# An adaptive-norm block on one core: the opening of the first batch in a written-out issue order

## The chip, the core and the metric

The kernel runs on one core of one Trainium2 chip. The metric is the device time of one execution in microseconds (us), from the first to the last instruction with what lies around them; lower is better. All data are 32-bit floats. The engines are called TensorE (PE in the profile, its weight loads PEld), VectorE (DVE), ScalarE (ACT), GpSimd (POOL) and SyncE (SP). SyncE only issues transfers here; ScalarE and GpSimd issue some too.

## The reference

There are four batches of 512 tokens with 512 channels. In short:

```python
mod = (silu(c) @ wmod).reshape(4, 6, 1, 512)          # sa, ca, ga, sb, cb, gb
h = layernorm(x) * (1 + ca) + sa
q = silu(conv4(h @ Wq)); k = silu(conv4(h @ Wk)); v = silu(conv4(h @ Wv))   # 6 heads, 64/64/128
beta = sigmoid(h @ Wb); g = -exp(A_log) * softplus(h @ Wa + dt_bias)
o = gated_delta_rule(l2norm(q) * 64**-0.5, l2norm(k), v, g, beta)           # a scan over tokens
x = x + ga * ((rmsnorm(o) * norm_weight * silu(h @ Wg)) @ Wo)
h = layernorm(x) * (1 + cb) + sb
x = x + gb * ((silu(h @ w_gate.T) * (h @ w_up.T)) @ w_down.T)
```

## The kernel before

**Tiling.** A matrix of tokens and channels is held channels first, 128 channels by 512 tokens, so that one projection to 128 output channels is four accumulating matrix products with 512 columns (`projected`, L424). The profile counts each of them twice, so a whole projection shows as x8.

**Who sets the order.** The program is written against a framework with a scheduler: it knows the data dependencies, gives every instruction a priority from the place in the program, and writes one fixed order for each engine. On the chip each engine takes its instructions strictly in that order and waits where an operand isn't there. Tiles come from pools with a few buffers for each tag; a new tile waits until the oldest of its tag is done with. The tags that matter: `fill` and `seq` (three PSUM banks each), `w` (four projection weights), `acc` (four 128x512 results), `wm` (one buffer, for the later modulation weights and then for the weight sums), `sq` (one buffer).

**The opening of batch 0**, as the program has it:

- `modulation(*modulation_load(j))` for j = 1 and 0 (L227): the 1 MB weight is loaded on ScalarE's queue, multiplied (L188), copied from PSUM by VectorE (L190), reduced and turned over the channels by small products (L194), and added into `mod_t` (L195).
- `load_x(0)` on SyncE's queue; the sentinel writes of `far` into `gd` (L248, eight small transfers) also on SyncE's.
- `normed_t(0)`: statistics (L276, L277), the root on ScalarE (L286), normalising (L289, VectorE), 16 transposes (L295), and four scaled copies to `ht` on ScalarE (L296).
- `keys`, `queries`, `values` of batch 0: for each of 3 + 3 + 6 projections `conv_silu` does the product (L424), a scaled copy on ScalarE (L432), three tap additions on VectorE (L434) and the activation on ScalarE (L438). For keys and queries, `squares` follows (L444 on ScalarE, L450 on TensorE, L451).
- `decays` and `stored`: the decay gates of the delta rule, some thirty tiny VectorE operations, ending in a store to `gd`.
- `load_x(1)` and `load_x(2)` on ScalarE's queue; `normed_t` of both comes after `triangles(0)` in the program.

**What follows.** `triangles(0)` reads `gd` back (`ec`, L532), scans and exponentiates it, multiplies it onto products of the keys (L574, L578), stores the result (`ad`, L581), loads it in another layout (`pm`, L588) and inverts 96 small triangles in thirty dependent VectorE steps (L598, L602). The inverse is stored (`td`, L606) and read back as `t` (L651), and the first product of `delta_rule(0)` needs it (L659). The matrix products that fill TensorE during `delta_rule(0)` are `keys` and `queries` of batches 1 to 3 (`rest`). Later modulations run one at a time in `step`, between values: a 1x1 copy by GpSimd (`after`, L171) holds the load back, and L188, L190, then L194 or L198 follow.

**Weight sums.** `weight_sums` makes combinations of the feed-forward weights, sixteen times in sequence through the single `wm` buffer: load (L803, SyncE's queue), four sums on GpSimd (L808 to L811), store (L812). The weights of the projections of batches 1 to 3 are loaded on the same SyncE queue (L210), in between.

The line that puts the inversion ahead of everything for batch 0:

```python
with tc.high_priority(-LATER if b else 0):
```

Of the kernel before, what the change touches and what calls it, by code (L numbers as in the profile page):

```python
# [7 lines left out]

F32 = mybir.dt.float32
# [6 lines left out]
P = 128  # L16
# [21 lines left out]
def adaln_block(  # L38
# [40 lines left out]
    def fill(name):  # L79
        return bank("fill", 3, name)  # L80
# [76 lines left out]
    warm = const.tile([P, 1], F32, name="warm")  # L157
    act.activation(warm, eps, AF.Silu)
    act.activation(sc_t[:, :, :B], c_in, AF.Silu)

# [23 lines left out]
    def modulation(j, wm):  # L184

        pm = fill(f"pm{j}")
        for k in range(KD):
            pe.matmul(pm[k * S : (k + 1) * S, :], sc_t[:, k, :], wm[:, k, :], start=True, stop=True)  # L188
        part = pa_.tile([P, D], F32, tag="acc", bufs=4, name=f"part{j}")
        vec.tensor_copy(part, pm)  # L190
        if j in MOD:
            pt = fill(f"pmt{j}")[:, : KD * B].rearrange("p (t b) -> p t b", b=B)
            for t in range(KD):
                pe.matmul(pt[:, t, :], part[:, t * P : (t + 1) * P], fold[:, :B], start=True, stop=True)  # L194
            vec.tensor_scalar_add(mod_t[:, MOD[j]], pt, 1.0 if j in (1, 4) else 0.0)  # L195
            return
        pg = fill(f"pmg{j}")[:B, :]
        pe.matmul(pg, fold[:, :B], part, start=True, stop=True)  # L198
        val = pa_.tile([P, D], F32, tag="acc", bufs=4, name=f"val{j}")[:B]
        vec.tensor_copy(val, pg)  # L200
        mag = pa_.tile([P, D], F32, tag="acc", bufs=4, name=f"mag{j}")[:B]
        vec.scalar_tensor_tensor(mag, val, -1.0, val, ALU.mult, ALU.max)
        vec.tensor_scalar(val, val, 0.0, 2.0, ALU.is_ge, ALU.mult)
        vec.tensor_scalar_add(val, val, -1.0)
        vec.scalar_tensor_tensor(mag, mag, 0.25, val, ALU.max, ALU.mult)
        pool.dma_start(gate_d[j // 3], mag)

    def weight(src, col, nm):
# [4 lines left out]
    def load_x(b):  # L213
        ts = []
        if b == 2:

            room = w1.tile([P, NT, D], F32, tag="hf", bufs=2, name=f"xt{b}")
        for c in range(NT):
            if b == 2:
                t = room[:, c, :]  # L220
            else:
                t = pa_.tile([P, D], F32, tag="xt", bufs=4, name=f"xt{b}_{c}")
            (act if b else sp).dma_start(t, x[b, c * P : (c + 1) * P, :])
            ts.append(t)
        return ts

    for j in (1, 0):  # L227
        modulation(*modulation_load(j))
    first_w = weight(w_k, 0, "k0_0")
    xts = load_x(0)  # L230
    wab = const.tile([P, KD, S], F32, name="wab")
# [3 lines left out]
    for nm, src, n in (("k", conv_k, NP), ("q", conv_q, NP), ("v", conv_v, H)):  # L235
        cw[nm] = const.tile([P, n, TAPS], F32, name=f"conv_{nm}")
        sp.dma_start(cw[nm], src.rearrange("(n p) i -> p n i", p=P))
    neg_a = const.tile([P, H], F32, name="neg_a")
    sp.dma_start(neg_a, a_log.partition_broadcast(P))
    act.activation(neg_a, neg_a, AF.Exp)  # L240
    pool.tensor_scalar(neg_a, neg_a, -1.0, None, ALU.mult)
    dtb = const.tile([P, H], F32, name="dtb")
    sp.dma_start(dtb, dt_bias.partition_broadcast(P))
    nw = const.tile([P, 1], F32, name="nw")
    sp.dma_start(nw, norm_weight.rearrange("(p o) -> p o", o=1))
    for t in gd:
        for a in range(2):
            sp.dma_start(t[a, 0, :, :, 0:1], far)  # L248

# [67 lines left out]
    def decays(bs, hts):  # L317

        m = len(bs)
        n = f"{bs[0]}"  # L320
# [17 lines left out]
        ab = pa_.tile([P, T], F32, tag="acc", bufs=4, name=f"ab{n}")[:rows]  # L338
        act.copy(ab, pab[:rows])
        pat = (seq if bs == [0] else fill)(f"pat{n}")  # L340
        for c in range(NT):
# [12 lines left out]
        for i in range(m):  # L354
# [3 lines left out]
            )  # L358
        act.activation(beta, pv[:, :, :, H : 2 * H].rearrange("p b c h -> p b h c"), AF.Exp, scale=-1.0)
        flat = [v.rearrange("p b h c -> p (b h c)") for v in (z, e, t, t2, s, beta)]  # L360
        fz, fe, ft, ft2, fs, fb = flat
        vec.tensor_scalar_add(fb, fb, 1.0)
        vec.reciprocal(fb, fb)


        vec.scalar_tensor_tensor(fe, fz, -1.0, fz, ALU.mult, ALU.max)
        act.activation(fe, fe, AF.Exp, scale=-1.0)
        vec.tensor_scalar_add(ft, fe, 2.0)
        vec.reciprocal(ft, ft)
        vec.tensor_mul(ft, ft, fe)  # L370
        vec.tensor_mul(ft2, ft, ft)
        vec.tensor_scalar_mul(fs, ft2, 1.0 / 17.0)
        for q in (15.0, 13.0, 11.0, 9.0, 7.0, 5.0, 3.0):
            vec.scalar_tensor_tensor(fs, fs, 1.0 / q, ft2, ALU.add, ALU.mult)
        vec.scalar_tensor_tensor(fs, fs, 1.0, ft, ALU.add, ALU.mult)
        vec.tensor_scalar_max(fz, fz, 0.0)
        vec.scalar_tensor_tensor(fs, fs, 2.0, fz, ALU.mult, ALU.add)
        g, y = gy[:, :, 0], gy[:, :, 1]
        for i in range(m):
# [3 lines left out]
            vec.tensor_scalar_max(g[:, i], g[:, i], G_FLOOR)  # L383
        return beta, lambda: stored(bs, m, n, gy, g, y)

    def stored(bs, m, n, gy, g, y):

        pd = (seq if bs == [0] else fill)(f"pd{n}")
        hc = H * NT
        for i in range(m):  # L390
            pe.matmul(
                pd[:, i * hc : (i + 1) * hc], upto, g[:, i].rearrange("p h c -> p (h c)"),
                start=True, stop=True,
            )
        act.activation(
            y.rearrange("p b h c -> p b (h c)"), pd[:, : m * hc].rearrange("p (b c) -> p b c", b=m),
            AF.Exp,
        )
        for i, b in enumerate(bs):
            for par in range(2):  # L400
                r = slice(par * C, (par + 1) * C)
                pool.tensor_copy(y8[b][r, :, par::2], y[r, i])
            pgt = (seq if bs == [0] else fill)(f"pgt{b}")
            pe.transpose(pgt[: 2 * hc, :P], gy[:, i].rearrange("p a h c -> p (a h c)"), ident)
            gyt = pa_.tile([P, T], F32, tag="acc", bufs=4, name=f"gyt{b}")[: 2 * hc, :P]
            act.copy(gyt, pgt[: 2 * hc, :P])
            act.dma_start(
                gd[b].rearrange("a g h c i -> (g h c) a i")[:, :, 1:],
                gyt.rearrange("p (a i) -> p a i", a=2),
            )  # L410

    tails, pending = [], []

# [12 lines left out]

    def conv_silu(w, taps, col, ht, nm):

# [4 lines left out]
        for i in range(1, TAPS):  # L433
            vec.scalar_tensor_tensor(  # L434
                acc[:, i:], pp[:, : T - i], taps[:, col, TAPS - 1 - i : TAPS - i], acc[:, i:],
                ALU.mult, ALU.add,
            )
        act.activation(acc, acc, AF.Silu)  # L438
        return acc

    def squares(t, dst, p, scale, nm):

        sq = pa_.tile([P, T], F32, tag="sq", bufs=1, name=f"sq_{nm}")
        act.activation(sq, t, AF.Square)  # L444
        pn = fill(f"pn_{nm}")
        pv = pn[:, : NT * 2].rearrange("p (c u) -> p c u", u=2)
# [6 lines left out]
        )  # L453

    def keys(bs, hts):
        if bs == [0]:
            betas, store = decays(bs, hts)
        sk = {}
        for i, b in enumerate(bs):
            sk[b] = pa_.tile([P, H, NT], F32, tag=f"sk{i}", bufs=1, name=f"sk{b}")  # L460
        for p in range(NP):
            w = first_w if bs == [0] and p == 0 else weight(w_k, p, f"k{bs[0]}_{p}")
            for b in bs:
# [3 lines left out]
                lagging(lambda a=(kt, sk[b], p, 1.0, n): squares(*a))  # L467
            if p == 1 and bs != [0]:
                betas, store = decays(bs, hts)
            if p == (1 if bs == [0] else 2):  # L470
                store()
        def scalars():
            for i, b in enumerate(bs):
                act.activation(nk[b], sk[b], AF.Sqrt)
                pool.tensor_scalar(nk[b], nk[b], -1.0, None, ALU.mult)
                vec.reciprocal(sc[b], sk[b])
                vec.scalar_tensor_tensor(sc[b], sc[b], -1.0, betas[:, i], ALU.mult, ALU.mult)

        lagging(scalars)

# [8 lines left out]

    def values(bs, hts):  # L490
        for h in range(H):
            w = weight(w_v, h, f"v{bs[0]}_{h}")
# [530 lines left out]
    ending, count = [], [0]  # L1023
    hts = {0: normed_t(0, xts)}
    keys([0], hts)
    queries([0], hts)
    rest = list(range(1, B))
    xts = {b: load_x(b) for b in rest[:2]}
    loaded = []

# [5 lines left out]

    steps.extend(lambda j=j: step(j) for j in range(2, 7))
    values([0], hts)
    triangles(0)
    for b in rest[:2]:  # L1040
        hts[b] = normed_t(b, xts[b])
    gates([0], hts)
# [78 lines left out]
```

## Time and profile before

| | us |
|---|---|
| median of three runs | 1316.91 |
| lowest, highest | 1315.91, 1321.75 |
| span of the profiled execution | 1315.2 |
| TensorE busy in it | 1234.9 |
| VectorE, ScalarE, GpSimd busy | 733.7, 383.5, 290.8 |

No separate time is given for the profiled execution; its span is 1.7 us below the median of the runs, and 0.7 us below the lowest.

The page of the profile shows each engine's busy time, then the span in 40 equal slices (a digit is the busy share in tenths, 32.9 us to a slice; PEclk is TensorE's granted clock in tenths of full speed), then the chain that ended last and the costliest groups. The trace behind it answers finer questions: busy time in given stretches, who waited for whom, and the instructions in order of time. A line of the last kind has start, duration, engine, source line, operation, output<-input, shape and count; what stands in brackets is idle time before it and what ended it. The order of the instructions on each engine can be read from the program of either kernel.

### The profile page before, as it was taken

The numbers are of one execution on the slowest core, as the hardware profiler recorded it, in microseconds if no ns is written. First come the engines' busy times: TensorE is split into PE (matmuls) and PEld (weight loads), VectorE is DVE, ScalarE is ACT, GpSimd is POOL, SyncE is SP. The second block draws the span as 40 slices with busy tenths as digits, with TensorE's granted clock in tenths as the row PEclk, the third lists the DMA queues.
The fourth block names the chain that finished last, engine by engine and source line by source line (L and its number), as shares of the span: only waits on it lengthen the run. The fifth ranks groups of instructions, "written<-read, shape, count | busy, mean of one in ns | idle before, by whom it ended". The sixth has DMA issues, their size and how long they took to land.

```text
span 1315.2 us, 18413 instructions
## 1 busy us (share of the span) xinstructions
PE 1234.9 (94%) x6752; PEld 807.1 (61%) x6752; DVE 733.7 (56%) x1574; ACT 383.5 (29%) x740; POOL 290.8 (22%) x357
## 2 busy tenths in 40 slices
PE   6799898999889998999999999799999999999998
PEld 3345355554344565767757666666666578888884
DVE  3665865656188255784445558543555543563564
ACT  2633355554142354211103332101134312112110
POOL 4100214533210012030023121233111221131113
PEclk9799898999899999999999999899999999999999
DMA  7579667667874537664436555544632555444431
GB/s 209 138 203 288 186 173 209 172 212 249 255 205 126 144 98 176 199 202 139 134 113 189 124 126 165 161 130 150 193 85 70 174 186 175 146 152 152 140 114 62
DMA packets 217945, 214.57 MB, mean 163 GB/s; under 512 B 95608, under 2 KB 164216, under 8 KB 217856
## 3 DMA queue, kind: packets, MB, share of 16 engines
q1 hardware_dynamic: 194976, 176.58, 46.4%
q10 hardware_dynamic: 19360, 17.93, 4.2%
q0 software_dynamic: 3520, 18.89, 3.8%
q8 instruction: 54, 0.88, 0.3%
q14 instruction: 35, 0.29, 0.1%
HBM read 159.23 MB, written 50.97 MB: 160 GB/s over the span
## 4 chain that ended last, share of the span: by engine, by line
PE 64%; DVE 14%; DMA 11%; POOL 5%; issue 3%; ACT 2%; SPq 1%; POOLq 0%; DVEq 0%; ACTq 0%
PE phg L960 14%; PE phu L960 11%; PE pd L847 9%; PE pwo L745 5%; PE pds L890 4%; PE pp_v L424 3%; PE pp_g L424 3%; PE pm L704 2%; DVE ti L602 2%; PE scratch L631 2%; DMA wsum<-wsg 2%; DVE tip L598 2%; DMA wsum<-wsu 2%; PE pp_q L424 1%; PE pp_k L424 1%
## 5 line engine op out<-in xcount | busy, mean ns | idle before, releaser
L847 PE MATMUL pd<-wdn,hid 128*128 128x512 f32 x320 | 140.6, 592 | 0.0
L960 PE MATMUL phg<-hf,wg 128*128 128x256 f32 x512 | 138.4, 387 | 1.8 <-DMA wg<-wsum 1.8
L960 PE MATMUL phg<-hs,wg 128*128 128x256 f32 x384 | 103.6, 390 | 5.9 <-DVE hid L967 5.8
L960 PEld LDWEIGHTS phg<-hf,wg 128*128 128x128 f32 x512 | 95.9, 192 | 20.7 <-issue 6.3
L960 PE MATMUL phu<-hf,wu 128*128 128x256 f32 x384 | 101.1, 388 | 2.2 <-DMA wu<-wsum 2.0
L847 PEld LDWEIGHTS pd<-wdn,hid 128*128 128x128 f32 x320 | 60.7, 190 | 68.1 <-issue 63.6
L960 PE MATMUL phu<-hs,wu 128*128 128x256 f32 x384 | 95.6, 382 | 2.5 <-DVE up L973 2.5
L424 PE MATMUL pp_g<-ht,wg 128*128 128x512 f32 x192 | 91.6, 617 | 5.7 <-DMA wg<-in_w_g_dram 4.6
L853 POOL TENSOR_TENSOR xm<-xm,tmpf 128x512 f32<-128x512 f32 x40 | 50.9, 1273 | 206.8 <-DVE tmpf L852 206.8
L424 PE MATMUL pp_v<-ht,wv 128*128 128x512 f32 x192 | 89.3, 609 | 3.5 <-DVE v L503 2.3
L745 PE MATMUL pwo<-wo,ot 128*128 128x512 f32 x192 | 91.8, 608 | 0.0
L965 ACT COPY hid<-phg 128x256 f32<-128x256 f32 x32 | 11.9, 372 | 247.9 <-PE phg L960 247.9
L960 PEld LDWEIGHTS phg<-hs,wg 128*128 128x128 f32 x384 | 71.5, 193 | 20.4 <-DVE hid L967 8.3
L960 PEld LDWEIGHTS phu<-hs,wu 128*128 128x128 f32 x384 | 71.9, 191 | 19.2 <-DVE up L973 7.1
L960 PEld LDWEIGHTS phu<-hf,wu 128*128 128x128 f32 x384 | 71.7, 192 | 15.5 <-issue 3.1
L424 PEld LDWEIGHTS pp_g<-ht,wg 128*128 128x128 f32 x192 | 35.1, 195 | 43.0 <-issue 41.8
L852 DVE TENSOR_TENSOR tmpf<-pd,gb 128x512 f32<-128x512 f32 x40 | 27.5, 689 | 59.4 <-PE pd L847 44.7
L424 PEld LDWEIGHTS pp_v<-ht,wv 128*128 128x128 f32 x192 | 35.2, 193 | 41.5 <-issue 38.5
L989 ACT ACTIVATE hid<-hid 128x1024 f32<-128x1024 f32 x32 | 33.8, 1057 | 86.2 <-DVE hid L973 70.0
L434 DVE SCALAR_TENSOR_TENSOR acc_v<-pp_v,conv_v,acc_v 128x511 f32<-128x511 f32 (+2 forms) x72 | 53.4, 743 | 9.8 <-ACT acc_v L432 8.8
L704 PE MATMUL pm<-r,l 128*128 128x128 f32 x384 | 53.8, 285 | 1.0 <-ACT r L700 0.9
L704 PEld LDWEIGHTS pm<-r,l 128*128 128x128 f32 x384 | 48.2, 194 | 8.9 <-ACT r L700 4.7
(244 smaller groups left out, 2060.1 us busy)
## 6 DMA issues: line engine op xcount, KB each, us to landing
wdn<-in_w_down_t_dram SPq DMA_DIRECT2D x32, 512.0 KB, 4.3
wg<-wsum SPq DMA_DIRECT2D x32, 512.0 KB, 3.8
wu<-wsum SPq DMA_DIRECT2D x32, 512.0 KB, 3.6
wg<-wsum SPq DMA_DIRECT2D x32, 384.0 KB, 4.4
wu<-wsum SPq DMA_DIRECT2D x32, 384.0 KB, 4.3
wsum<-wsg POOLq DMA_DIRECT2D x8, 896.0 KB, 4.3
wsum<-wsu POOLq DMA_DIRECT2D x8, 896.0 KB, 4.6
vd<-v SPq DMA_DIRECT2D x24, 256.0 KB, 3.4
```

What stands on the lines that cost most here:

```text
L424: pe.matmul(pp, w[:, k, :], ht[:, k, :], start=(k == 0), stop=(k == KD - 1))
L434: vec.scalar_tensor_tensor(acc[:, i:], pp[:, : T - i], taps[:, col, TAPS - 1 - i : TAPS - i], acc[:, i:], ALU.mult, ALU.add,)
L598: vec.tensor_tensor(v, pm[:, j, j + 1 :, None].broadcast_to([n, m, j]), t[:, j : j + 1, :j].broadcast_to([n, m, j]), ALU.mult,)
L602: vec.tensor_add(t[:, j + 1 :, :j], t[:, j + 1 :, :j], v)
L704: pe.matmul(pm[:, h], l[:, hs.start + h, 2 * par : 2 * par + 2, :], r[:, par, hs.start + h], start=True, stop=True,)
L745: pe.matmul(pw, ot[:, h, :], wo[:, h, :], start=(h == 0), stop=(h == H - 1))
L847: pe.matmul(pd, hids[q, i // 2][:, i % 2, c * P : (c + 1) * P], wdn[q, i // 2][:, i % 2, :], start=(i == 0), stop=(i == NQ - 1),)
L852: vec.tensor_mul(tmp, pd, gb)
L853: pool.tensor_add(xm[c], xm[c], tmp)
L890: pe.matmul(o[:, c], l[:, c * P : (c + 1) * P], r, start=j == 0, stop=j == 1)
L960: pe.matmul(o, l[:, k], r[:, k], start=k == 0, stop=k == 1)
L989: act.activation(hid, hid, AF.Silu)
```

## The change

- The opening of batch 0, from the modulation to the third value projection, becomes a function `opening` inside a region in which the order on TensorE, VectorE and ScalarE is the order of the text. GpSimd's and SyncE's order is still the scheduler's.
- Both early modulation loads are issued on ScalarE's queue ahead of its first table load. The x tiles of batch 0 go ahead of the first key weight on SyncE's queue, the second key weight ahead of the small constants.
- 24 transposes of the identity (`idle`) are put at TensorE's start, and one-element activations that load the tables of Sqrt and Silu early.
- Of modulation 0, ScalarE copies the result from PSUM; of batch 0, ScalarE normalises two of four x tiles, and VectorE makes two of four `ht` copies.
- The keys start at once; the decays are cut into pieces (generators) of which one follows each projection. The activation of a projection is issued one projection late, the sums of squares two late. Transposes of values (`by_token`) start after the region.
- The x tiles of batches 1 to 3 are loaded by GpSimd's queue, for batches 1 and 2 held back by eight 1x1 copies until the fifth projection; their normalising is held behind the last tap of the region on VectorE (`issue_after`). The eight sentinel writes go to GpSimd's queue.

```diff
+    def opening():
+        order = tc.manual_schedule(engines={EngineType.PE, EngineType.DVE, EngineType.Activation})
+        with order:
+            loads = [modulation_load(j) for j in (1, 0)]
+            act.activation(warm, eps, AF.Silu)
+            act.activation(sc_t[:, :, :B], c_in, AF.Silu)
+            act.activation(warm, eps, AF.Sqrt)
+            idle = seq("idle")
+            for i in range(24):
+                pe.transpose(idle[:, (i % 4) * P : (i % 4 + 1) * P], ident, ident)
...
+            for (j, wm), copy in zip(loads, (vec.tensor_copy, act.copy)):
+                pm = seq(f"pm{j}")
+                for k in range(KD):
+                    pe.matmul(pm[k * S : (k + 1) * S, :], sc_t[:, k, :], wm[:, k, :], start=True, stop=True)
+                part = pa_.tile([P, D], F32, tag="acc", bufs=4, name=f"part{j}")
+                copy(part, pm)
+                if j:
+                    for c in range(2):
+                        statistics(pa_, xts[c], mv[:, c, :])
+                    by_channel(j, part, seq(f"pmt{j}"))
+                    for c in range(2, NT):
+                        statistics(pa_, xts[c], mv[:, c, :])
...
+            for i in range(len(nms) + 1):
+                if i < len(nms):
+                    accs[i] = conv(w, cw[nm], p, ht, nms[i])
+                j = i - 1
+                if j >= 0:
+                    act.activation(accs[j], accs[j], AF.Silu)
+                    if j < 2 * NP:
+                        act.dma_start((kd if j < NP else qd)[0][:, j % NP, :], accs[j])
+                        sqs[j] = squared(accs[j], nms[j])
+                    else:
+                        tails.append(lambda a=(0, j % NP, accs[j]): by_token(*a))
+                if i:
+                    next(decay, None)
+                if i == 4:
+                    xts_ = {b: load_x(b) for b in (1, 2)}
+                j = i - 2
+                if 0 <= j < 2 * NP:
+                    squares_sum(sqs[j], (sk, eq[0])[j // NP], j % NP, (1.0, float(DK) * EPS)[j // NP], nms[j], seq)
...
-    hts = {0: normed_t(0, xts)}
-    keys([0], hts)
-    queries([0], hts)
+    hts, xts = opening()
+    opened = taps_end[0].ins
+    for t in gd:
+        for a in range(2):
+            pool.dma_start(t[a, 0, :, :, 0:1], far)
...
-    values([0], hts)
+    between(1)
+    values([0], hts, NP)
     triangles(0)
-    for b in rest[:2]:
-        hts[b] = normed_t(b, xts[b])
+    with tc.issue_after(opened):
+        for b in rest[:2]:
+            hts[b] = normed_t(b, xts[b])
```

## The prediction

> **What bounds the kernel now.** First the busy totals and slices of the page.
>
> ```profile
> span 1315.2 us, 18413 instructions
> PE 1234.9 (94%) x6752; PEld 807.1 (61%) x6752; DVE 733.7 (56%) x1574; ACT 383.5 (29%) x740; POOL 290.8 (22%) x357
> ```
>
> TensorE is the bound: 94% busy, 80 us idle. The slices show the idle time thickest in the first 66 us (digits 6 and 7). Next, busy time by stretches of the opening; columns: stretch, us, busy us (count) of PE, PEld, DVE, ACT, POOL, then granted clock, DMA share, GB/s.
>
> ```profile
> 0.00:6.50 6.50, 0.00 (x0) 0.00 (x0) 0.00 (x0) 1.70 (x3) 5.41 (x27) 1.00 0.68 213
> 6.50:24.00 17.50, 12.73 (x55) 7.54 (x56) 7.68 (x17) 5.86 (x8) 9.18 (x26) 1.00 0.80 224
> 33.00:45.00 12.00, 8.82 (x47) 4.36 (x46) 10.76 (x38) 9.02 (x12) 0.62 (x2) 0.80 0.30 90
> 45.00:55.00 10.00, 4.23 (x23) 2.16 (x21) 5.03 (x8) 4.59 (x7) 0.00 (x0) 0.67 0.61 131
> 55.00:66.00 11.00, 11.00 (x45) 5.01 (x46) 6.60 (x11) 8.29 (x11) 3.38 (x4) 0.74 0.84 196
> ```
>
> Nothing runs on TensorE until 6.5; at 33 to 45 VectorE is the busy one (10.76 of 12); at 45 to 55 TensorE works 4.23 of 10, and the granted clock is down to 0.67. Third, whom TensorE waits for until 120 us (total, times, longest):
>
> ```profile
> PE pn_k L450 <- ACT sq_k L444: 8.3, 3, 5.8
> PE pm L188 <- DMA wm<-in_w_mod_dram: 6.5, 1, 6.5
> PE pmt L194 <- DVE part L190: 4.9, 4, 3.5
> ```
>
> The key squares stand behind other work on ScalarE; TensorE, in order, stands with them. Last, the instructions in order of time, for landmarks.
>
> ```profile
> 23.89 1.13 PE L424 MATMUL pp_k<-ht,wk 128*128 128x512 f32 x2
> 78.73 3.60 PE L424 MATMUL pp_v<-ht,wv 128*128 128x512 f32 x8
> 161.26 0.33 SPq L606 DMA_DIRECT2D td<-ti  x1
> 169.16 0.30 PE L659 MATMUL scratch<-t,at 64*64 64x32 f32 x2 [1.34 <-DMA t<-td]
> 341.28 1.91 SPq L803 DMA_DIRECT2D wsg<-in_w_gate_t_dram  x4
> 343.79 0.45 SPq L210 DMA_DIRECT2D wg<-in_w_g_dram  x1
> 348.99 6.26 PE L424 MATMUL pp_g<-ht,wg 128*128 128x512 f32 x8 [4.65 <-DMA wg<-in_w_g_dram]
> ```
>
> The first projection begins at 23.9, the third value projection ends at 78.4, the inverted triangles go out at 161.26 and their first reader starts 7.9 us later.
>
> I carry one number through: the lead of the changed kernel at each landmark.
>
> **To the first projection (23.9).** The order stays: weight (6.5), product 1.9, copy 0.7 (9.1), four statistics at 0.8 each (13, with the last x tile landing by about 12; before, they landed from 7.9 to 10), root, reciprocal and offset 0.6 (14; the 1.28 us table load at 6.83 is now early), two normalisings of 0.54 on each of two engines (15), 16 transposes and one small product, `ht` copy 0.8. The 24 idle transposes (0.134 to 0.233 apart, so 3 to 6 us) lie in TensorE's empty 6.5 us and cost nothing; without that cover they would cost their length. Their worth is the clock: at full clock the 16 transposes and the product take 2.1 + 1.05, at half 3.7 + 1.85. So the first projection begins at 18.6 to 21; I take 19.5, a lead of 4.4. Does a transpose warm the clock? Three restarts before rise to full clock 5.3, 6.7 and 5.6 us after activity begins (41.7, 53.9, 150.5); at the start, products are fast from about 24.0, 1.5 us after the first wide projection (22.48) but 5.8 after the transposes began at 18.2. That row says they count.
> The Trainium skill ("TensorE: Matmul & The Clock Gate", Part 4: PE-mode transpose) says the opposite: full clock doesn't engage for transposes, as they don't count as busy in the same way. By it the idle ones are useless, and the first projection would start at 21 to 23.
> Both modulation weights on one queue at once compete with x. In the row of 6.5 to 24 the DMA engines are 0.80 busy, so there is room, and the second megabyte is only needed by the last `mod_t`.
> The Trainium skill ("DMA: Bandwidth & Descriptors", Issuing engines are not separate DMA queues) says that transfers of all issuers share the same 16 engines, which speaks against starting more at once; by it x would land at 10 to 12, and no row of the trace before has both weights under way from the start.
>
> **Nine projections in a written order.** Each takes 3.63 us at full clock; with six sums of squares (0.57 net), `pab` 1.06, `pat` 0.5, `pd` and stray products 0.6 that is 38.3 us, so the third value projection ends near 58 instead of 78.4. For each projection VectorE has three taps (0.74 each, 2.2, and small ones), ScalarE copy 0.69, activation 0.63, square 0.63 (1.95), both under 3.6. Removed: the 8.3 us of waits and the half-clock stretches (41 to 47, 51 to 61; a group of 16 `pp_q` products took 10.0 instead of 7.2). Lead 20.
>
> **Where it is given back.** After the region TensorE has one more projection, two `pvt`, then `pm` and `pmg` of the next modulation. Its load goes out at about 62.5, after the ScalarE work ahead of it, and lands 5.6 us later at 68: TensorE idles some 4.7. `pmg` then waits for a copy behind some 18 VectorE operations (statistics and normalising of batch 1, 0.5 to 0.7 each): 2.7 to 3.4, and a restart at half clock costs 2.5. The fifth value projection starts near 72.3 instead of 88.1: lead 16. Batch 1's and 2's statistics, which before partly lay in waits, now come in one lump before `ec` and the products `at` of the triangles; so the gate projection (104.6) comes at 95.6, lead 9, and the `pm` issue (114.4) at 105.8, lead 8.6. The eight sentinel writes took 5.1 and 3.0 us of SyncE's queue before, at 10.8 and 16.4, with the third key weight behind them at 19.5; that goes. GpSimd issues them and the x loads; its engine is free (5.41 + 9.18 us in the first 24, then nearly nothing), so they cost nothing there; if GpSimd were late, x of batch 1 would hold the lump.
>
> **The inversion and its first reader.** Before: the copy `ti` at 121.17, thirty levels until 161.26, 40.1 us because taps and copies lie between. A level uninterrupted takes 0.72 on average (21.7 in all), with copy 1.06 and the one modulation copy and the other small work now ordered among them about 3.4: 26.3. Starting at 112.5, `td` goes out at 138.8; 7.9 later, 146.7, its reader may start. But in the changed order only 2.25 projections of the rest stand ahead of that reader, where before there were 6, four sums of squares and 5 of 12 `pab`: 17.7 us of work (13.7 + 2.3 + some 2) still to be done. TensorE itself arrives there at about 146.5, so the wait is short. The reader leads by 22.5, less 17.7 owed: net 4.5.
>
> **The weight sums.** Sixteen rounds of about 12 us (load 2.9, sums 3.5, store 4.2, issue 1.9) run in sequence on SyncE, and the gate weight at 343.79 sits behind a round; TensorE loses 4.65 and then 2.6 at half clock. In the changed order that weight stands behind a round later in the sequence, and the rounds start only up to 8 us earlier, those bound to the stores of `delta_rule(0)` some 17. So the wait may vanish (7.3) or stay: I credit 4. Total lead 8.5: 1315.2 - 8.5 = 1306.7; the runs' median stands 1.7 above that span, so 1308.
>
> **Rivals.**
> - The opening's gain carries through: VectorE keeps ahead, the waits at 64 to 72 and in the gates don't arise, and 10 us more reach the end: about 1297. For it: VectorE is only 56% busy. Against: its operations in the order before the `pmg` copy.
> - The gain is given back: each wait above twice its size, or the gate weight as late as before: net lead 0 to 6, 1311 to 1317. For it: the chain of the triangles is longer than TensorE's work beside it.
> - Slower: the inversion comes late. TensorE stands at the first use of `t` with 17.7 us less done. The sign turns where `td` goes out after 161.26 - 17.9 = 143.3, only 4.5 us later than I forecast. If the levels are interrupted as before (40.1 from 112.5: 152.6), the loss is 9.3 us: about 1326. For it: before, most of that chain is interruption. Against: in the changed order just some ten other operations stand among the levels.
> - The idle transposes don't do what they are for: then 2 to 4 us less; inside my range.
>
> **How the numbers follow.** About 0.5%, 6.6 us, is what a measurement of this kernel can tell from no change. Forecast (1300 to 1310) 0.40; carried through 0.12; given back 0.31; slower by the inversion 0.17. Faster by over 6.6 us (below 1310.3) is the first two, 0.52; the third is the same; the last slower. The range leaves out the extremes: 1297 to 1322.
>
> **What the changed profile would show.** Right: first projection at 18.6 to 21, `pp_v` of the third value projection ending at 56 to 61, no wait for `sq_k`, a wait for `wm` near 63 to 68, `td` issued at 136 to 142, the reader of `t` with a short wait, no 4.65 us wait for the gate weight near 340. Wrong: `td` after 143, a wait of over 5 us at `t`, transposes still 0.233 apart at 17, or a new half-clock stretch in the rest's keys.

## The result, and the profile after

The changed kernel takes 1335.95 us in the median of four runs (1330.16 to 1339.75), the one before 1318.28 (1315.91 to 1321.75): a ratio of 1.013, 95% interval 1.0092 to 1.0169. Measured again beside other kernels (e5 below) it is 1.0194 (1.0135 to 1.0253). It is slower by more than the 0.5% that counts. Executions of one and the same kernel lie up to 1% from their median here, so ratios are told with their intervals, and what is read from a single profile is good to some 4 us for a landmark and 8 us for the time of the whole rest.

The page after: 17.5 us more span, of which 7.4 are more busy time of TensorE and 10.1 more idle time.

```profile
span 1332.7 us, 18506 instructions
PE 1242.3 (93%) x6776; PEld 811.3 (61%) x6776; DVE 740.6 (56%) x1574; ACT 394.7 (30%) x750; POOL 301.3 (23%) x389
PE   8976899789989999889999999899999999999997
PEclk8978899789989999999999999899999999999999
```

Busy time by stretches, cut at the changed kernel's landmarks: start, first projection (20.0), end of the opening (62.6, the first transposed values), gates (99.2), first key of the rest (145.0), first use of `t` (157.4). Columns as in the prediction.

```profile
6.50:20.00 13.50, 9.57 (x49) 6.12 (x49) 6.16 (x16) 3.14 (x6) 12.71 (x33) 0.68 0.81 227
20.00:62.60 42.60, 42.60 (x205) 20.14 (x206) 25.20 (x58) 22.89 (x37) 5.99 (x19) 0.98 0.56 179
62.60:99.20 36.60, 26.58 (x185) 14.56 (x183) 29.33 (x55) 17.56 (x25) 7.79 (x17) 0.77 0.68 178
99.20:145.00 45.80, 33.67 (x115) 15.59 (x115) 33.71 (x91) 7.89 (x13) 1.57 (x4) 0.85 0.95 234
145.00:157.40 12.40, 7.95 (x18) 3.29 (x18) 7.66 (x11) 3.65 (x6) 3.13 (x4) 1.00 0.75 221
```

The nine projections, and the fourth value projection behind them, run without a gap (42.60 busy of 42.60). Then TensorE idles 10.0 of 36.6 and 12.1 of 45.8 us, at a granted clock of 0.77 and 0.85. The same two stretches of the kernel before:

```profile
78.30:104.60 26.30, 23.24 (x173) 13.18 (x172) 18.03 (x30) 9.26 (x15) 1.24 (x4) 1.00 0.80 213
104.60:136.80 32.20, 29.36 (x117) 13.90 (x115) 20.05 (x56) 10.35 (x15) 0.72 (x2) 1.00 0.98 298
```

Idle 3.1 and 2.8, the clock full: 58.5 us where it is now 82.4, although the two stretches of before hold one value projection more (3.6 us) and 20 products of 64x64 less (0.4): for the same products it was some 55. Whom TensorE waits for until 160 us in the changed kernel (total, times, longest):

```profile
PE pp_g L442 <- DMA wg<-in_w_g_dram: 5.6, 1, 5.6
PE pm L187 <- DMA wm<-in_w_mod_dram: 4.7, 1, 4.7
PE scratch L780 <- DMA t<-td: 4.5, 1, 4.5
PE pmg L194 <- DVE part L189: 3.4, 2, 2.5
PE pm L501 <- DMA wm<-in_w_mod_dram: 3.0, 2, 2.5
PE scratch L752 <- DVE yk L763: 2.1, 2, 1.2
```

The wait for the key squares (8.3) is gone; a row of smaller ones behind the opening stands in its place. The instructions in order of time:

```profile
19.99 7.98 PE L442 MATMUL pp_k<-ht,wk 128*128 128x512 f32 x16 [0.23 <-ACT ht L536]
59.22 3.60 PE L442 MATMUL pp_v<-ht,wv 128*128 128x512 f32 x8
68.88 1.93 PE L187 MATMUL pm<-wm,sc_t 128*32 128x512 f32 x8 [4.68 <-DMA wm<-in_w_mod_dram]
111.08 1.10 SPq L709 DMA_DIRECT2D pm<-ad  x1
112.60 3.86 SPq L213 DMA_DIRECT2D wg<-in_w_g_dram  x4
120.98 8.66 PE L442 MATMUL pp_g<-ht,wg 128*128 128x512 f32 x16 [5.58 <-DMA wg<-in_w_g_dram]
147.24 0.33 SPq L727 DMA_DIRECT2D td<-ti  x1
157.44 0.30 PE L780 MATMUL scratch<-t,at 64*64 64x32 f32 x2 [4.49 <-DMA t<-td]
371.32 6.34 PE L442 MATMUL pp_g<-ht,wg 128*128 128x512 f32 x8 [5.00 <-DMA wg<-in_w_g_dram]
```

The landmarks beside the forecast:

| | before | forecast | after | lead |
|---|---|---|---|---|
| first projection | 23.9 | 19.5 | 20.0 | 3.9 |
| third value projection ends | 78.4 | 58 | 59.2 | 19.2 |
| fifth value projection | 88.1 | 72.3 | 73.5 | 14.6 |
| first gate | 104.6 | 95.6 | 99.2 | 5.4 |
| `pm` issued | 114.4 | 105.8 | 111.1 | 3.3 |
| first key of the rest | 136.8 | 138.3 | 145.0 | -8.2 |
| `td` issued | 161.3 | 138.8 | 147.2 | 14.1 |
| first use of `t` | 169.2 | 146.7 | 157.4 | 11.8 |
| span | 1315.2 | 1306.7 | 1332.7 | -17.5 |

(138.3 is the forecast's 146.5 for TensorE's arrival at `t`, less 2.25 projections of 3.63.) The opening did what was forecast to 1.2 us. From the end of the third value projection to the first key of the rest 27.4 us of lead are lost (19.2 to -8.2), and from there to the end of the program 9.3: 1187.7 instead of 1178.4.

### The profile page after: what moved, and what is told of

The parts are those of the page before. It is cut to its first block, busy times and chain, and to the rows that moved or that the text cites. A ratio compares the mean times of both kernels' runs of the same rounds, so it can differ in the third digit from the quotient of the medians.

```text
span 1332.7 us, 18506 instructions
## 1 busy us (share of the span) xinstructions
PE 1242.3 (93%) x6776; PEld 811.3 (61%) x6776; DVE 740.6 (56%) x1574; ACT 394.7 (30%) x750; POOL 301.3 (23%) x389
## 4 chain that ended last, share of the span: by engine, by line
PE 64%; DVE 15%; DMA 8%; issue 5%; POOL 4%; ACT 2%; SPq 1%; POOLq 0%; DVEq 0%; ACTq 0%
PE phg L1081 14%; PE phu L1081 11%; PE pd L968 9%; PE pp_v L442 5%; PE pwo L866 5%; PE pds L1011 4%; PE pp_g L442 3%; PE pp_q L442 2%; DVE ti L723 2%; DVE tip L719 2%; PE pm L825 2%; PE pp_k L442 2%; PE scratch L752 1%; DMA wsum<-wsg 1%; PE pf L816 1%
## 5 line engine op out<-in xcount | busy, mean ns | idle before, releaser
L1081 PEld LDWEIGHTS phg<-hf,wg 128*128 128x128 f32 x512 | 95.7, 191 | 19.2 <-issue 4.9
L442 PE MATMUL pp_g<-ht,wg 128*128 128x512 f32 x192 | 95.1, 637 | 10.7 <-DMA wg<-in_w_g_dram 10.6
L1086 ACT COPY hid<-phg 128x256 f32<-128x256 f32 x32 | 11.9, 372 | 247.8 <-PE phg L1081 245.5
L442 PE MATMUL pp_k<-ht,wk 128*128 128x512 f32 x96 | 51.5, 666 | 4.9 <-ACT beta L377 4.6
```

Of the source, the lines that this page charges most:

```text
L442: pe.matmul(pp, w[:, k, :], ht[:, k, :], start=(k == 0), stop=(k == KD - 1))
L1081: pe.matmul(o, l[:, k], r[:, k], start=k == 0, stop=k == 1)
```

## The experiments

Two numbers are read from every profile, as they hold the same work of TensorE in every kernel (but for the idle transposes and at most 16 small products in e9 to e12): F, the time at which the first key of the rest begins, and R, from there to the end. A is the part of F behind the opening, from the first transposed values on; it holds the same work in the changed kernels, to 38 small products, and one projection more in the one before. Before: F 136.8, A 58.5, R 1178.4; changed: F 145.0, A 82.4, R 1187.7. "Ahead" is how many projections of the rest stand ahead of the first use of `t`. The theory: what the opening gains is lost because TensorE stands at `t` with work still owed. Its rivals: the order of loads on SyncE, the held loading of x with its lump on VectorE, the late decays, the crowd of transfers. A profile is of one execution, which can be far from the median: those of e1 and e3 are the fastest of their ten (6.9 and 8.5 us under the median), those of e2 and e8 are 4.5 and 10.3 over it. The ratios decide; F, A and R say where to look. Code that is left out is marked by three dots.

**The changed kernel again.**

> The changed kernel as it is, beside the next three on one chip: 1.010 to 1.016 of the time before. In its profile again a wait of 4 to 6 us for a gate weight near 115 to 121, and a wait for t near 155.

Ratio 1.0194 (1.0135 to 1.0253), above what was expected; F 142.1, A 78.8, R 1195.4; both waits are there, 5.2 for the gate weight and 4.0 ahead of `t`. So one order gives F and R that differ by 3 to 8 us between profiles.

**Keys first** (theory: the work still owed when TensorE stands at `t`).

```diff
-    delta_rule(0)
     keys(rest, hts)
+    delta_rule(0)
```

> The changed kernel with keys(rest) ahead of delta_rule(0) in the program: by the order of the program 24 more products of projections of the rest (6 projections instead of 2.25), 32 more of the sums of squares and all 12 pab stand ahead of the first use of t, as before the change; the opening, the modulations and the gates stay. Changed kernel: 1336; before: 1317 to 1318. If the loss is the work still owed when TensorE stands at t (17.7 us, of which 12 to 18 weren't taken up by delta_rule(0)): 1316 to 1324, and TensorE doesn't wait at t. If the loss is in the order of loads ahead of the gates (13.6 us), or in the loading of x, nothing of this changes: 1333 to 1338, or the saved wait at t of 4.5 alone: 1331.

Ratio 1.0098 (1.0061 to 1.0134); ahead 6; F 137.5, A 77.0, R 1182.0. TensorE's wait at `t` is gone. R falls by 5.7 against the first profile of the changed kernel and 13.4 against the second. The order up to the gates is the changed kernel's, and A is nearly as long (77.0; 78.8 and 82.4): this edit mends only what comes behind. The ratio lies where the expectation put the saved wait at `t` alone (1331, or 1.010), above the 1316 to 1324 for the owed work, and its interval overlaps that of the first measurement (1.0092 to 1.0169). More than the wait isn't shown.

**The gate weights' queue, and the early modulation.**

```diff
-        sp.dma_start(t, src[:, col * P : (col + 1) * P].rearrange("(k p) f -> p k f", p=P))
+        (eng or sp).dma_start(t, src[:, col * P : (col + 1) * P].rearrange("(k p) f -> p k f", p=P))
...
-            w = weight(w_g, h, f"g{bs[0]}_{h}")
+            w = weight(w_g, h, f"g{bs[0]}_{h}", act if bs == [0] else None)
```

> The changed kernel with the six gate weights of batch 0 issued on ScalarE's queue instead of SyncE's, where the last four stood behind the store and reload of the products of the triangles (issued at 112.6, needed at 107). The scheduler then also puts 6 projections of the rest ahead of the first use of t. If the order of loads on SyncE makes the loss: no wait for wg at 115 to 121 (5.6), no restart at half clock (about 3) and with it 1322 to 1329, and the rest of the gain of the opening as well if the owed work is no cause: 1316. If only the owed work makes it: as keys first, 1316 to 1324. If neither (x, the modulation ahead of the triangles): 1332 or more.

Ratio 1.0013 (0.9977 to 1.0050), not to be told from the kernel before; ahead 6; F 142.2, A 78.1, R 1178.7. The wait for the gate weight is gone:

```profile
114.12 9.89 PE L442 MATMUL pp_g<-ht,wg 128*128 128x512 f32 x16
126.49 1.07 PE L187 MATMUL pm<-wm,sc_t 128*32 128x512 f32 x8
129.82 1.77 PE L194 MATMUL pmg<-part,fold 128*4 128x512 f32 x2 [2.27 <-DVE tip L719]
168.00 0.30 PE L780 MATMUL scratch<-t,at 64*64 64x32 f32 x2
```

Yet the 16 products take 9.89 instead of 7.1 (half clock), `pmg` waits 2.27 for a copy inside the inversion, and A is no shorter. Here `td` goes out at 160.8, 13.6 later than in the changed kernel, without any wait at `t`. In these profiles what it regains lies in R, with 6 projections ahead. The run ties the moved queue to another order behind, so it doesn't price the queue alone.

```diff
-    between(1)
     values([0], hts, NP)
```

> The changed kernel without the step of the modulation that the change puts ahead of the fourth value projection; each later modulation moves one place back. The wait for wm at 64 to 69 (4.7, and some 2.5 of half clock behind it) goes, and one held load less stands on SyncE ahead of ex and the stores of the triangles. If these loads set the start of the inversion (120): it starts 4 to 7 earlier and the time is 1327 to 1331. If the owed work decides, the time gained waits at t again or is owed there: 1333 to 1338.

(Taken out of the changed kernel, whose gate weights stay on SyncE.) Ratio 1.0091 (1.0055 to 1.0127); ahead 2; F 140.9, A 77.9, R 1175.7. The wait for `wm` is gone and the gates begin at 93.8, but 47.2 us pass from there to the first key (45.8 in the changed kernel); the second of the three groups of products of the triangles now waits 6.9. The inversion starts at 114.4 (120.1 in the changed kernel, but 118.9 and 114.3 in e5 and e1, whose order up to there is the same), and TensorE doesn't wait at `t`. The ratio is e1's with the work still owed, and R is the shortest of all: against the theory that owed work alone lengthens R, though this profile is the fastest of its ten.

> Both edits: gate weights of batch 0 on ScalarE's queue, and without the early step of the modulation. Here the first use of t stands after only 20.25 products as in the changed kernel (2.25 projections of the rest), so the queue is mended and the owed work is not. If the order of loads on SyncE alone makes the loss: at or below the time before, 0.990 to 1.001. If the owed work makes a part of its own: 1.004 to 1.012, with waits inside delta_rule(0) and more half clock between 160 and 330.

(Both edits at once.) Ratio 1.0273 (1.0223 to 1.0324), above both expectations; ahead 2.25; F 139.8, A 77.0, R 1204.6. The worst R, in an order in which the waits for `wm` and for the gate weight are mended. TensorE waits 6.17 at `t`, and far behind it, for a weight sum:

```profile
563.04 2.05 PE L1081 MATMUL phg<-hf,wg 128*128 128x256 f32 x4 [9.08 <-DMA wg<-wsum]
```

Only this kernel, e9 and e14 wait so long for a weight sum (5.2 at most in the others); why these three isn't shown.

> As the one before, and keys(rest) ahead of delta_rule(0), so that 6 projections of the rest stand ahead of t. If the owed work has a price of its own, this is 0.005 to 0.012 below the one before, and under the time before: 0.985 to 0.998. If not, the two are alike within 0.004.

Ratio 1.0080 (1.0049 to 1.0111); ahead 6; F 135.8, A 72.7, R 1190.7: 13.9 less than e6, but the 9.08 for the weight sum are gone with it, and the time isn't under that of the kernel before, as was expected of a price of the owed work.

> The kernel before with the six gate weights of batch 0 on ScalarE's queue. There the third weight was issued at 97.5, ahead of its use at 115, so that no wait of TensorE is removed: 0.997 to 1.002 if the place of the gate weights on SyncE matters only in the changed order; 0.985 to 0.993 if ScalarE's queue is better in any order, and then the third run above says little on the change.

(The kernel before with the same edit of the queue.) Ratio 1.0054 (1.0020 to 1.0088): no gain by this queue in the order before, rather a small loss.

**The loading of x and the hold.**

```diff
-            if b:
-                after(t[:1, :1])
-            (pool if b else sp).dma_start(t, x[b, c * P : (c + 1) * P, :])
+            (act if b else sp).dma_start(t, x[b, c * P : (c + 1) * P, :])
...
-    with tc.issue_after(opened):
...
```

> The changed kernel with x of the batches 1 to 3 on ScalarE's queue, without the copies that hold them, and their normalising without the hold behind the region. If the late loading by GpSimd or the lump of statistics on VectorE behind the region costs (pmg waits 2.5 and 0.9 for a copy behind them, x of batch 3 collides with the triangles' stores at 94 to 107): 1326 to 1331. If not: 1334 to 1338; if the early loads collide with the weights of the opening, up to 1342.

Ratio 1.0258 (1.0192 to 1.0325). The opening ends at 79.8 instead of 62.6, F 154.2. So the held loads and the held normalising are what lets the opening run through; the loss is above even the 1342 that the expectation allowed for it.

> The changed kernel without the hold of the normalising of batches 1 and 2 behind the last tap of the region (x is still loaded by GpSimd and held back). If the hold costs by the lump on VectorE: the statistics come earlier, gates at 93 to 97, 0.003 to 0.008 below the changed kernel. If the hold protects the region, the third value projection ends later (62 to 70 instead of 59) and the time is the same or longer, as with x on ScalarE's queue.

(Only the `issue_after` line is taken out.) Ratio 1.0188 (1.0121 to 1.0254); the opening ends at 73.8, A 78.0. The hold protects the region by some 10 us, and A is not shorter without it: the time is that of the changed kernel.

> The changed kernel with the normalising of batch 2 behind the gates of batch 0 in the program, so that half of the statistics that stand in a lump on VectorE at 60 to 85 (busy 9.84 and 9.30 of 10 at 60 to 80) go later. If that lump sets the gates: gates at 93 to 96 instead of 99, first key of the rest at 136 to 141. If not: gates at 98 to 100.

(`normed_t(2)` behind `gates([0])`.) Ratio 1.0223 (1.0153 to 1.0292). The lump does set the gates, which begin at 93.3, but the stretch from there on grows from 45.8 to 50.8: A 80.0. R is 1198.7, with the wait of e6 for a weight sum in it.

```profile
64.10:93.30 29.20, 22.39 (x161) 11.45 (x160) 24.80 (x48) 14.30 (x20) 6.10 (x13) 0.77 0.67 173
93.30:144.10 50.80, 36.56 (x139) 17.96 (x139) 37.18 (x96) 13.52 (x20) 6.39 (x12) 0.83 0.93 246
```

**The decays.** In the changed kernel their pieces follow one projection each, so `gd` is stored at 62.1, where before it was 46.0, and the scans of `ec` run at 75.9 to 83 instead of 55 to 59.

```diff
-                    next(decay, None)
+                    for _ in range({2: 2, 3: 3, 5: 2}.get(i, 1)):
+                        next(decay, None)
```

> The changed kernel with the pieces of the decays put earlier: 1, 2, 3, 1, 2 pieces after the first five projections of the region instead of one after each of nine. The decays reach gd some 8 to 13 us earlier (62.1 in the changed kernel, 46.0 before), so ec, its exponentials and the products of the triangles come earlier, and the scheduler puts two of three products of the triangles among the values and three gate weights ahead of the reload. If the late decays are what gives the lead back between 60 and 145: gates at 88 to 93 instead of 99, first key of the rest at 126 to 134 instead of 142 to 145. The first use of t then stands after only 1.25 projections of the rest, so the owed work remains: 1.003 to 1.012 of the time before. If the held modulation loads or SyncE's order bound that stretch whatever the decays do: first key of the rest at 140 or later and 1.012 to 1.02.

Ratio 1.0237 (1.0197 to 1.0276); ahead 1.25; `gd` at 54.2; opening ends at 67.2, F 148.9, A 81.7, R 1197.0. Earlier decays don't bring the lead back. With the products of the triangles pulled forward, the first gate weight stands behind them on SyncE and TensorE waits 7.5 for it:

```profile
99.76 2.62 SPq L703 DMA_DIRECT2D ad<-at  x3
102.42 5.39 SPq L213 DMA_DIRECT2D wg<-in_w_g_dram  x3
109.72 5.93 PE L442 MATMUL pp_g<-ht,wg 128*128 128x512 f32 x8 [7.49 <-DMA wg<-in_w_g_dram]
563.73 2.04 PE L1082 MATMUL phg<-hf,wg 128*128 128x256 f32 x4 [9.09 <-DMA wg<-wsum]
```

The last line is the wait of e6 again.

> Early decays and keys(rest) ahead of delta_rule(0): 9 projections of the rest and all pab stand ahead of t. If late decays and owed work are the two causes: first key of the rest at 126 to 134, the stretch from there to the first value projection of the rest 155 to 166 (changed kernel 179 to 183), and 0.985 to 0.996 of the time before. If only one of them is: 1.000 to 1.008.

Ratio 1.0147 (1.0105 to 1.0190), above both expectations; ahead 9; F 150.6, R 1190.3: 6.7 less than e9, and less than the 9.09 for a weight sum that e9 has and e10 hasn't.

> As the one before, without the early step of the modulation. If that step still costs with early decays (a wait of 4.7 for wm at 64 to 69): 0.003 to 0.005 below the one before; else the same within 0.004.

Ratio 1.0161 (1.0111 to 1.0211), F 149.0, R 1188.9: the same within 0.004.

> Early decays, keys first and the gate weights of batch 0 on ScalarE's queue. With early decays the first three gate weights stand ahead of the reload on SyncE already, so the queue should matter no more: within 0.004 of e10. If SyncE's order is a cause of its own: 0.004 to 0.008 below it.

Ratio 1.0128 (1.0086 to 1.0171), F 149.2, R 1188.0: the same within 0.004.

**Transfers, the clock, and all together.**

> The changed kernel with the 1.5 MB load of wo moved from SyncE at 116.5 into the region, after its second projection, on GpSimd's queue, where the DMA engines are busy 0.16 to 0.36 of the time (20 to 40). The order on TensorE stays (2.25 projections ahead of t). If the crowd of transfers at 94 to 130 (DMA share 1.05 to 1.09) is what makes the gates late: the wait for the third gate weight falls from 5 to 6 us to under 3, and the first key of the rest comes at 137 to 141 instead of 142 to 145. If the place of the gate weights behind the reload or VectorE's work does, nothing of it changes. Time 1.008 to 1.019 either way, as the owed work stays.

Ratio 1.0113 (1.0044 to 1.0182); F 139.5, A 78.9, R 1184.9. F lies in the range of the first expectation, but because this opening ended 2 us earlier (60.6): the wait for the gate weight is still 5.4, and the four stores of `ad` still hold SyncE 11.7 us (11.5 in the changed kernel). It isn't the 1.5 MB of `wo`.

> The changed kernel without the 24 transposes of the identity. If they warm the clock for the first product of the modulation only (1.06 us instead of 1.93 before) and the wait for the second weight at 9.5 to 12 lets it fall again: first projection at 20 to 21.5 and no change of the time that can be told, within 0.004. If transposes keep the clock up until the first projection: 21.5 to 23.5.

Ratio 1.0129 (1.0046 to 1.0211); R 1186.6; first projection at 20.0 with or without the transposes. First the rows without them, then those of the changed kernel:

```profile
6.68 1.93 PE L498 MATMUL pm<-wm,sc_t 128*32 128x512 f32 x8 [6.68 <-DMA wm<-in_w_mod_dram]
12.02 1.94 PE L498 MATMUL pm<-wm,sc_t 128*32 128x512 f32 x8 [0.68 <-DMA wm<-in_w_mod_dram]
```

```profile
1.74 4.24 PE L492 MATMUL idle<-ident 128*128 128x128 f32 x24 [1.74 <-POOL ident masks.py:199]
6.51 1.06 PE L501 MATMUL pm<-wm,sc_t 128*32 128x512 f32 x8 [0.53 <-DMA wm<-in_w_mod_dram]
11.99 1.93 PE L501 MATMUL pm<-wm,sc_t 128*32 128x512 f32 x8 [2.50 <-DMA wm<-in_w_mod_dram]
```

> All at once on the changed kernel: gate weights of batch 0 on ScalarE's queue, no early step of the modulation, batch 2 normalised later, wo loaded early, keys(rest) ahead of delta_rule(0) (6 projections ahead of t). Each alone left the stretch from the first transposed values to the first key of the rest at 77 to 82 us (before: 58.5). If several waits share that stretch and each hides the next: with all gone 60 to 68, first key of the rest at 123 to 131, and 0.985 to 0.998 of the time before. If one thing that none of them touches bounds it (the chain of modulations through one buffer, or of the triangles): 73 to 80 again, first key at 136 or later, and 1.000 to 1.008.

Ratio 1.0054 (1.0022 to 1.0086); ahead 6; F 138.7, A 74.8, R 1182.3. All three numbers meet the second expectation: something that none of the five edits touches bounds most of this stretch. Undone together they take 4 to 8 us off A, where the first expectation had it at 60 to 68.

> The kernel of e2 (gate weights of batch 0 on ScalarE's queue; 6 projections ahead of t by the scheduler's own order) with wo loaded early. If the two mended causes add up: 0.993 to 1.001 of the time before, at or under e2's 1.001. If the order behind is what decides, anything from 1.000 to 1.010.

Ratio 1.0031 (0.9994 to 1.0069); ahead 6; F 134.1, A 73.6, R 1185.9. It isn't under e2, so the two edits don't add up. No version beats the kernel before; the nearest are this one and e2.

## Why the prediction was wrong

**Right.** The nine projections (38.3, measured 39.2), the wait for `wm` behind them (4.7, measured 4.68), the fifth value projection (72.3, measured 73.5), and the inversion itself (26.3 from copy to store, measured 27.2). The opening gains what it promised.

**Right by luck: the first projection (19.5, measured 20.0).** The idle transposes do warm the clock (last section), but the written order puts the second modulation ahead of the first transposes, and TensorE waits 2.50 for its weight at 12.0; its product then runs at half clock, 1.93, and so do the transposes, still 0.21 to 0.25 apart at 17.8 to 19.3, a sign that the prediction gave of being wrong. Without the idle ones the first projection comes at the same time (e16). The sum said that the second megabyte is only needed by the last `mod_t`; in this order it isn't.
The Trainium skill ("DMA: Bandwidth & Descriptors", Issuing engines are not separate DMA queues) has transfers of all issuers share the engines; the trace agrees: the last statistics of batch 0 waited for x until 11.9, where x had landed at about 10 before.

**Wrong: from the opening's end to the first key.** The forecast had the lead fall from 20 to -1.5 by a list of waits; it fell to -8.2. The terms missed or too small:
- The gate weights. The sum followed `pm<-ad` on SyncE and not what is queued behind it. Four of the six gate weights were: issued at 112.6, the first of them needed at 115.4. TensorE waits 5.58 and then takes 8.66 for 16 products, 1.5 more than at full clock.
- The stores of `ad`. Their four issues took SyncE 11.5 us (1.7 in all before), behind a modulation load for which SyncE stood 6.6 us and two loads of `ex` that took 10.9 and 13.2 us to land. The forecast took the old duration, so `ti` starts at 120.1 instead of 112.5. This alone doesn't make A long: in e9 to e12 the stores took 3.0 to 4.7, and A stayed at 81.

```profile
95.82 11.49 SPq L702 DMA_DIRECT2D ad<-at  x4
```

- The clock. One restart of 2.5 us was priced; 0.77 and 0.85 over 82 us are worth 15.3 us of full clock, part of it while idle. Busy time for the same products grew by some 11 us (60.3, where before 52.6 hold a projection more).

Told as a sum, the 27.4 us are some 16 more idle time of TensorE (22.1 instead of 5.9) and some 11 of slower products.

No single wait of this stretch is the cause. Whatever was undone, singly or together, A stayed between 72.7 and 81.7 (e1, which doesn't touch it, has 77.0): a wait that goes is followed by another, as the gates of e14 and the product of the triangles in e3 show. VectorE's busy time in it grew from 38.1 to 63.0 us, but it has idle time too, and moving a part of its work (e14, e17) didn't bring A down to what it was. What bounds the rest of the way down to 58.5, or 55 for the same products, stays open.

**Wrong: the wait at `t`, and the owed work at its bare price.** The step "22.5, less 17.7 owed: net 4.5" takes for granted that TensorE hardly waits at `t` and that the owed work costs no more than its 17.7. Measured, the reader's lead is 11.8; less 17.7 that is -5.9, and the end is at -17.5. From the first use of `t` to the end the changed kernel takes 1175.3 us, the one before 1146.0: 29.3 more, where the step has 17.7. So the 26.0 us between the forecast lead of 8.5 and the measured -17.5 are 10.4 lost up to the reader, 11.6 behind it, and the credit of 4 for the weight sums.

The 11.6 can be placed. From F to the first use of batch 1's `t`, with 4650 to 4652 products of TensorE left in each kernel, it takes 299.2 us before, 310.8 and 314.4 in the two profiles of the changed kernel, 300.1 in e1, 298.7 in e2 and 297.9 in e3. The loss of R lies in this stretch, and it goes with keys(rest) ahead (e1) as well as with the work still owed (e3). What these three share is that TensorE doesn't wait at `t`. Over the changed kernels, R is 1175.7 to 1182.3 where it doesn't wait there and at most 6 projections are ahead (e1, e2, e3, e17), and 1184.9 to 1204.6 wherever it waits 2.5 us or more (to 1196.7 without e6, e9 and e14 and their weight sum); e7, e10 and e11, which wait at most 0.9, have 1188.9 to 1190.7. That is an order in single profiles, good to some 8 us, and no run changes the wait alone: that it makes the loss is argued, not shown.

What owed work costs beyond the wait isn't shown either. Where keys(rest) alone was put ahead, R fell three times: by 5.7 and 13.4 (e1 against the two profiles of the changed kernel), by 13.9 (e7 against e6), by 6.7 (e10 against e9). But the first is what the saved wait at `t` would give, and in the other two pairs the wait of 9.1 us for a weight sum, some 400 us behind `t`, is in the one kernel and not in the other.

How a fixed order can lose time behind `t` can be seen at 227 to 238 in the changed kernel, where the decays of the rest come late:

```profile
227.71 0.69 PE L353 MATMUL pat<-ident,ab 96*128 96x96 f32 x4
234.66 1.26 POOL L869 TENSOR_TENSOR xr<-xr,tmpa 128x512 f32<-128x512 f32 x1
235.96 0.69 DVE L277 BATCH_NORM_STATS2 st<-xr 128x6 f32<-128x512 f32 x1 [7.25 <-POOL xr L869]
236.81 1.28 ACT L377 ACT_TABLE_LOAD   x1 [8.02 <-DVE z L366]
238.39 2.08 PE L442 MATMUL pp_k<-ht,wk 128*128 128x512 f32 x2 [4.63 <-ACT beta L377]
```

GpSimd adds `xr` only behind a weight sum, VectorE's statistics stand behind `xr`, the last `z` of the decays behind those, ScalarE's exponential behind `z`, and TensorE behind ScalarE. Before, the products `pat` ran at 173.8. That GpSimd's sums pin this chain is argued from these rows; it was not tried.

**Wrong: the weight sums' credit of 4.** The wait for a gate weight is still there, 5.00 at 371.32 (4.65 before).

**The rivals.** The slower one had the right place and sign: `td` went out after 143.3, at 147.2. By its rule that costs 3.9, a span of 1319; the loss is 17.5. Its own number, 1326, is the nearest on record, but it came from an inversion of 40.1 us, which measured 27.2. Its mechanism is too narrow: in e2 `td` goes out at 160.8 and nothing waits, as 6 projections stand ahead. The time of `td` has to be read against what the fixed order puts ahead of its reader.

## What to carry to other kernels

An opening that runs without a gap can give its lead back where things that ran under its old gaps (here statistics, loads, the triangles' input) must now run behind it: list them before the gain is credited. When a wait is forecast on an in-order queue, follow everything queued behind it on that queue, and price each restart of TensorE at half clock. If a changed step moves a scheduler's order, count how much ready work stands ahead of each late operand. And when one edit makes a pair of kernels differ, look where in the program the difference lies: in two of three pairs here most or all of it was a wait some 400 us behind the place that the edit was meant for.

## What the runs showed of the hardware

- Transposes warmed TensorE's clock. After 24 of them (1.74 to 5.98) the first modulation product took 1.06 us, without them 1.93, at half clock (e16). The Trainium skill ("TensorE: Matmul & The Clock Gate", Part 4: PE-mode transpose) says that they don't count as busy in the same way; here they did. Behind a gap of 2.50 us it was lost again: the next product took 1.93.
- An issue can hold its engine's queue. The first 96 KB store of `ad` kept SyncE for 7.46 us and took 12.2 us to land (0.30 to 0.52 and at most 6.8 for the four of the kernel before), while the core moved 300 GB/s. The two loads of `ex` issued just before it landed only at 104.5 and 107.5. Moving 1.5 MB out of that time (e13) didn't shorten it. Why the queue was held isn't shown.
